# A two-layer graph attention kernel: separate buffers for background work, smaller stream tiles, a second list of late work

## The chip, the cores and the metric

The kernel runs on one core of a Trainium2 chip. The metric is the device time of one execution in microseconds: 3223.64 us as the median of three runs of the kernel before (3218.17 to 3225.19). The profile is of an execution with a span of 3218.2 us.

## What is computed

There are N = 2708 nodes with 1024 features each and a dense 0/1 adjacency matrix of 2708 x 2708. Everything is float32. Both layers start from a normalized and rectified copy of x and add their result to x:

```python
# layer 0
h = max(layernorm(x), 0)
f, g = h @ Wf + bf, h @ Wg + bg
e = relu(f @ g.T)
attention = softmax(where(adj > 0, e, -9e15), axis=1)
x = x + attention @ (h @ W + bW)
# layer 1
h = max(layernorm(x), 0)
hw = h @ W1
e = leaky_relu(hw @ a1 + (hw @ a2).T, 0.2)
attention = softmax(where(adj > 0, e, -9e15), axis=1)
x = x + relu(attention @ hw)
```

## The kernel before

**Tiling.** The nodes are cut into 21 full tiles of 128 rows and a rest of 20; the tiles go in pairs (NQ = 10 pairs and one pair of left-overs, MONO and TINY). The columns of the attention matrix, which are the rows of the result, are cut into five panels p of 512 to 576 columns. For each panel of layer 0 the kernel forms B = (Wf Wg') applied to the panel's h (`project_q`), the scores of all nodes against the panel (`scores`), their softmax, the aggregation of h by the weights (`aggregate` for panel 0, `aggregate_quartered` for the others), and a product with W (`project`). Layer 1 needs no score products: it builds the weights from two vectors (`weights1`), then aggregates and projects in the same way.

**Seven products.** Each big matrix product is done by a scheme of seven half-size products (M1 to M7) in place of eight, at the price of sums and differences of blocks. `aggregate_quartered` applies the scheme a second time inside five of the seven products (`BY_QUARTERS`); those inner products are `product` at L1030 and read two things from memory: blocks of h (`hr_d`) and precomputed sums of quarter blocks (`hs2_d`, called hs_d in the profile, as `hs_d` of the scores is too). Each inner product reads one tile "hc2" of 640 KB (five blocks of 256 columns, 5 KB in each partition).

**Sums made in the background.** The sums of quarters are made by `put_quarters` (L381): a load of four blocks ("hq", 512 KB), four VectorE operations into a second tile ("hq2"), and a store. There are 25 such items in each layer (five products, NK = 5 blocks each). `sums_h` (L353) makes first-level sums of h in the same manner from two tiles "hr" per pair, in place. `prepare_W` (L1284) loads rows of W ("w_rows"), sums them and stores the sums to `wt_d`. `raise_max` (L1325) updates running column maxima of layer 1 from a mask tile loaded by `load_mask` ("maskl", a slot).

**Queues and orders.** All loads are issued on SyncE, held in program order by `load` (L137). All stores are issued on GpSimd. Background work is a list, `later`: an item has a price in microseconds of VectorE, an optional fetch (its load) and an action. The main loops call `behind(us)`, which earns credit (capped at twice `us`) and runs items while credit is positive; `one` first issues the fetches of the next `ahead[0]` items (2 for most of the program, 1 during the first aggregation), then the first item's action. `flush` runs the whole list. `scores` calls `behind` after M6, M5, M2, M7, once with double rate after M3, and once after M4 of the previous pair; its rate is 1.0 for panel 1 and 0.65 from panel 2 on. While `nc.hold` names VectorE, as in `scores`, its operations too keep program order.

**Buffers.** On-chip memory is drawn from pools. `slots` has 53 buffers of 576 columns (score tiles S, B, T1, masks and temporaries). `strm` has ten buffers of 5 KB in each partition, as large as the largest tile asked of it, and serves every stream: As (operands of the scores), hc and hc2, md, w, adj_i (adjacency blocks), hsT, hT (four tiles per panel, L674), and the background's hq, hq2, hr and w_rows. A new tile takes a buffer that is free or waits for the last access of an older one; for a tile that is stored, that is the landing of the store. Since SyncE keeps program order, a load that waits for its buffer holds back all later loads.

**Order of the work around the change.** Panel 0's scores run while h is still being made (`make_pairs`, tiles hsT in the stream pool). Then come project_q(1), with `sums_h` behind it, aggregate(0, 0), with `sums_h` and `prepare_W` behind it, and scores of panel 1, with the 25 quarter sums of layer 0 behind it. For p from 1 to 4 come project(0, p-1), aggregate_quartered(0, p), project_q(p+1) and scores(p+1). Finished rows of layer 0 put new items for layer 1 on `later`. Before the last projection of layer 0 stands a `flush()` (L1686). In layer 1, `take_shifts(p)` (L1766) flushes and then takes the column maxima.

Of the kernel before, what the change touches and what calls it, by code (L numbers as in the profile page):

```python
# [8 lines left out]
FP = mybir.dt.float32  # L9
# [9 lines left out]
P = 128  # L19
W = 512  # L20
# [5 lines left out]
M1, M5, M6, M7, M3, M2, M4 = range(7)  # L26
# [4 lines left out]
BY_SCORES = (M1, M6, M5, M2, M7, M3, M4)  # L31
# [26 lines left out]
def kernel(  # L58
# [19 lines left out]
    nc = InOrder(tc)  # L78
    N, D = x.shape
    NC = D // P  # L80
    NH = NC // 2
# [4 lines left out]
    NM = P // 2  # L86
# [38 lines left out]
    def slot(name, shape=(P, WX), dt=FP):  # L125
        return slots.tile(list(shape), dt, tag="slot", name=name)

    def stream(name, shape=(P, D), dt=FP):
        return strm.tile(list(shape), dt, tag="strm", name=name)

    def in_16(o, i):

# [4 lines left out]
    def load(o, i):  # L137
        for a, b in in_16(o, i):
            tc.keep_in_program_order(nc.sync.dma_start(a, b))  # L139

    def store(o, i):
        for a, b in in_16(o, i):
            nc.gpsimd.dma_start(a, b)  # L143
# [43 lines left out]
        (nc.vector.tensor_copy if flip[0] else nc.scalar.copy)(o, i)  # L187


    later, credit = [], [0.0]  # L190
    ahead = [5]

    def put(us, go, fetch=None, takes_psum=False, ready=None):
        later.append([us, fetch, go, takes_psum, ready])

    def one():
        for it in later[:ahead[0]]:
            if it[1]:
                it[1]()
                it[1] = None  # L200
        us, _, go = later.pop(0)[:3]
# [179 lines left out]
    def put_quarters(l, m, k):  # L381

        two = []

        def fetch():
            two.append(stream("hq", (P, 4, WH)))
            load(two[0], hr_d[l][:, m, :, :, k].rearrange("p h f c -> p (h f) c"))

        def go():
            a11, a12, a21, a22 = (two[0][:, i] for i in range(4))  # L390
            o = stream("hq2", (P, 4, WH))
            s1, s2, s3, s4 = (o[:, i] for i in range(4))
            add(s1, a21, a22)
            sub(s2, s1, a11)
            sub(s3, a11, a21)
            sub(s4, a12, s2)
            store(hs2_d[l][:, m, :, k], o)
            made_quarters[l, m] = made_quarters.get((l, m), 0) + 1
        put(1.7, go, fetch)

    def quarters_until(l, m):
        while made_quarters.get((l, m), 0) < NK:
            one()

    u = consts.tile([P, NC], FP, name="u")
    v = consts.tile([P, NC], FP, name="v")
# [101 lines left out]
            one()  # L508


    def load_rows(w, c, name):
        t = stream(name)
        load(t, w[c * P:(c + 1) * P, :])
        return t

# [152 lines left out]
    def project_q(p, then={}):  # L668

        w = width[p]  # L670
        h = w // 2
        halved = lambda t: [t.rearrange("p (c i) -> p c i", c=NH)[:, 2 * g:2 * g + 2] for g in range(2)]
        lo, hi = ((halved(t) for t in first_h) if p == 0 else
                  ([stream("hT", (P, 2, WX)) for _ in range(2)] for _ in range(2)))  # L674
        o = 0
        for t, n in pieces[p]:
            if p == 0:
                break
            for e, side in enumerate((lo, hi)):
                for g in range(2):  # L680
                    s, cs = side[g][:, :, o:o + n], slice(2 * g, 2 * g + 2)
                    if t == TINY:
                        nc.scalar.copy(s, tinyT[:, e, cs, :NY])
                    elif t == MONO:
                        load(s, hsl_d[:, e, cs, NM:])
                    else:
                        q, k = pair_of[t]
                        load(s, hs_d[q][:, (BY_SCORES.index(M4 if k else M2) if e else 7 if k else BY_SCORES.index(M1)), cs])
# [5 lines left out]
        for g in range(2):  # L694
            sub(lo[g][:, :, h:w], hi[g][:, :, h:w], lo[g][:, :, h:w])

        def second():
            for g in range(2):
                sub(lo[g][:, :, :h], hi[g][:, :, h:w], T1[g][:, :, :h])

        def fourth():
            for g in range(2):
                sub(hi[g][:, :, :h], hi[g][:, :, :h], lo[g][:, :, :h])

        B = [in_pairs(f"B{m}") for m in range(7)]
        m1, m15, u2 = in_pairs("m1"), in_pairs("m15"), in_pairs("u2")
# [13 lines left out]
            return L[m][k][:, d * P:(d + 1) * P]  # L720

        def right(m, k):
            t, s = {M1: (lo, lo_), M2: (hi, lo_), M3: (hi, hi_), M5: (T1, lo_), M6: (lo, lo_), M7: (lo, hi_), M4: (hi, lo_)}[m]
            return t[k // 2][:, k % 2, s]

        def plus(o, a, bias, b):
            nc.vector.scalar_tensor_tensor(o, a, bias, b, op0=OP.add, op1=OP.add)
# [248 lines left out]
    def aggregate_quartered(l, p, S, sm, then={}, rate=3.0, fine=1.2):  # L976
# [33 lines left out]
            f_, b = i  # L1010
            return operand(m, 2 * k + f_)[:, b * hb:(b + 1) * hb]

        sums = {}

        def quarter_sums(m):

# [10 lines left out]
        def inner_right(m, n, k):  # L1027
            return sums[m, k][n] if n in sums[m, k] else part_of(m, k, {M1: (0, 0), M2: (1, 0), M3: (1, 1)}[n])

        def product(m, n, ps, start):  # L1030
            quarters_until(l, m)
            t = stream("hc2", (P, NK, WH))
            if n in (M1, M2, M4):
                load(t, hr_d[l][:, m, int(n == M4), int(n != M1)])
            else:
                load(t, hs2_d[l][:, m, {M5: 0, M6: 1, M7: 2, M3: 3}[n]])
            for k in range(NK):
                for d in range(2):
                    nc.tensor.matmul(ps[:, d], t[:, k, d * P:(d + 1) * P], inner_right(m, n, k),  # L1039
                                     start=(start and k == 0 and d == 0), stop=(k == NK - 1), skip_group_check=True)  # L1040
            behind(fine)

# [722 lines left out]

    def take_shifts(p):  # L1766
        flush()
        got["zm"] = shifts1(p)

    def take_weights(p):  # L1770
# [39 lines left out]
```

## Time and profile before

| What | Value |
|---|---|
| time, median of 3 | 3223.64 us |
| span of the profiled execution | 3218.2 us |
| mean granted TensorE clock | 0.973 |
| DMA traffic | 802.41 MB, mean 249 GB/s |
| hq loads and stores | 50 of 512 KB each; stores land 6.2 us after their issue (median) |
| hc2 loads | 280 of 640 KB |
| hT loads | 64 of 128 KB and 4 of 64 KB |

Each stage has its own limit. Busy time by stage, in microseconds, with the share of time in which the core's 16 DMA engines are busy:

| Stretch, us | Work | PE busy | VectorE busy | granted clock | DMA share |
|---|---|---|---|---|---|
| 212 to 372 | scores of panel 0 | 145.27 of 160 | 103.72 | 0.97 | 0.87 |
| 372 to 465 | project_q(1) | 73.67 of 93 | 68.80 | 0.89 | 0.72 |
| 465 to 640 | first aggregation | 156.98 of 175 | 92.75 | 0.97 | 0.86 |
| 640 to 860 | scores of panel 1 | 156.56 of 220 | 125.35 | 0.85 | 0.82 |
| 860 to 2145 | panels 1 to 4 of layer 0 | 1262.97 of 1285 | 930.37 | about 1 | about 0.83 |
| 2145 to 2262 | flush, last projection of layer 0 | 86.98 of 117 | 79.85 | 0.86 | 0.98 |
| 2262 to 3218 | layer 1 | 932.94 of 956.2 | 644.22 | 0.98 | about 0.73 |

In the page, PE is TensorE's matmuls, DVE is VectorE, ACT ScalarE, POOL GpSimd, and SP or SPq SyncE, whose instructions only issue transfers or wait. A line of waits names the engine, the tile and line that waited, what ended the wait, the total in microseconds, the number of times and the longest. A float32 matmul of the program appears as two in the profile, so one of the seven products of a pair in the scores, four matmuls in the code, shows as eight.

### The profile page before, as it was taken

The numbers are of one execution on the slowest core, as the hardware profiler recorded it, in microseconds if no ns is written. First come the engines' busy times: TensorE is split into PE (matmuls) and PEld (weight loads), VectorE is DVE, ScalarE is ACT, GpSimd is POOL, SyncE is SP. The second block draws the span as 40 slices with busy tenths as digits, with TensorE's granted clock in tenths as the row PEclk, the third lists the DMA queues.
The fourth block names the chain that finished last, engine by engine and source line by source line (L and its number), as shares of the span: only waits on it lengthen the run. The fifth ranks groups of instructions, "written<-read, shape, count | busy, mean of one in ns | idle before, by whom it ended". The sixth has DMA issues, their size and how long they took to land.

```text
span 3218.2 us, 43997 instructions
## 1 busy us (share of the span) xinstructions
PE 3014.6 (94%) x15606; PEld 2338.5 (73%) x15606; DVE 2184.8 (68%) x4956; ACT 478.5 (15%) x871; POOL 487.3 (15%) x704
## 2 busy tenths in 40 slices
PE   8998989866999999999999999996999999999998
PEld 4576667544669886788859887792765967969695
DVE  5765683655597466965688676985948567776853
ACT  3420020000030001200021000311313022131300
POOL 1420011211111001110041001112011011120102
PEclk9999999978999999999999999998999999999999
DMA  6999678888869787797778888799567757778787
GB/s 224 286 273 237 215 237 275 278 249 256 260 202 339 211 217 214 232 338 223 219 231 295 277 233 239 224 359 327 178 222 225 234 187 255 248 235 277 245 258 239
DMA packets 496714, 802.41 MB, mean 249 GB/s; under 512 B 175392, under 2 KB 330048, under 8 KB 496496
## 3 DMA queue, kind: packets, MB, share of 16 engines
q1 hardware_dynamic: 445136, 646.37, 65.4%
q0 software_dynamic: 51360, 153.24, 14.8%
q8 instruction: 124, 2.03, 0.3%
q14 instruction: 94, 0.77, 0.1%
HBM read 657.66 MB, written 141.78 MB: 248 GB/s over the span
## 4 chain that ended last, share of the span: by engine, by line
PE 63%; issue 16%; DMA 11%; DVE 5%; SPq 3%; POOL 2%; ACT 0%; POOLq 0%; DVEq 0%; ACTq 0%
PE sz L1365 7%; PE sx L1365 5%; PE gz L1039 5%; PE sy L1365 4%; PE pz L1246 4%; PE gy L646 4%; PE gx L646 4%; PE px L1246 3%; PE gy L1039 3%; PE gx L1039 3%; PE py L1246 3%; PE M_ps L559 3%; PE qz L646 3%; SPq L139 3%; PE qy L646 2%
## 5 line engine op out<-in xcount | busy, mean ns | idle before, releaser
L1365 PE MATMUL sz<-B,As 128*128 128x288 f32 (+2 forms) x1200 | 297.5, 398 | 10.6 <-DMA As<-hs_d 8.6
L1039 PE MATMUL gz<-quarter,hc 128*128 128x128 f32 (+2 forms) x2400 | 292.2, 279 | 6.7 <-DMA hc<-hs_d 4.5
L1039 PEld LDWEIGHTS gz<-quarter,hc 128*128 128x128 f32 x2400 | 282.4, 191 | 9.5 <-issue 5.0
L1365 PE MATMUL sx<-B,As 128*128 128x288 f32 (+2 forms) x800 | 214.5, 414 | 68.0 <-DMA As<-hs_d 63.6
L1365 PEld LDWEIGHTS sz<-B,As 128*128 128x128 f32 x1200 | 232.3, 194 | 60.4 <-issue 9.4
L1365 PEld LDWEIGHTS sx<-B,As 128*128 128x128 f32 x800 | 158.9, 200 | 107.0 <-DMA As<-hs_d 67.4
L1365 PE MATMUL sy<-B,As 128*128 128x288 f32 (+2 forms) x800 | 201.9, 396 | 3.4 <-DMA As<-hs_d 3.2
L646 PE MATMUL gy<-T,hc 128*128 128x288 f32 (+2 forms) x800 | 184.2, 391 | 0.0
L1365 PEld LDWEIGHTS sy<-B,As 128*128 128x128 f32 x800 | 153.6, 192 | 35.8 <-issue 3.9
L646 PEld LDWEIGHTS gy<-T,hc 128*128 128x128 f32 x800 | 152.0, 190 | 30.5
L1246 PE MATMUL px<-w,gT 128*128 128x512 f32 x320 | 143.6, 601 | 11.0 <-DMA w<-in_L_gnn_W_dram 11.0
L1246 PE MATMUL py<-w,ps 128*128 128x512 f32 x320 | 144.8, 602 | 6.0 <-issue 6.0
L1246 PE MATMUL pz<-w,ps 128*128 128x512 f32 x320 | 142.1, 594 | 0.8 <-DVE pt L45 0.8
L143 POOL DMA_DIRECT2D mk_d<-mask x55 | 36.1, 656 | 698.7 <-DVE mask L45 690.7
L1089 POOL TENSOR_TENSOR gT<-gT,rr 128x1024 f32<-128x1024 f32 (+5 forms) x16 | 61.0, 3813 | 531.7 <-DVE gT L45 531.7
L45 ACT COPY V<-gx 128x256 f32<-128x256 f32 (+2 forms) x80 | 30.4, 380 | 677.5 <-PE gx L1039 363.7
L45 DVE TENSOR_TENSOR V<-gz,V 128x256 f32<-128x256 f32 (+2 forms) x120 | 51.8, 432 | 115.3 <-PE gz L1039 115.1
L143 POOL DMA_DIRECT2D out_dram<-x_res x180 | 88.8, 500 | 242.5 <-DVE x_res L45 229.0
L45 ACT COPY sz<-sz 128x288 f32<-128x288 f32 (+2 forms) x5 | 1.9, 385 | 820.9 <-DVE acc L45 481.8
L1246 PEld LDWEIGHTS py<-w,ps 128*128 128x128 f32 x320 | 61.2, 193 | 82.7 <-issue 81.5
L1246 PEld LDWEIGHTS px<-w,gT 128*128 128x128 f32 x320 | 60.8, 193 | 82.7 <-issue 81.2
L1246 PEld LDWEIGHTS pz<-w,ps 128*128 128x128 f32 x320 | 60.2, 190 | 77.1 <-issue 71.6
(392 smaller groups left out, 5936.9 us busy)
## 6 DMA issues: line engine op xcount, KB each, us to landing
hc<-hs_d SPq DMA_DIRECT2D x160, 640.0 KB
As<-hs_d SPq DMA_DIRECT2D x150, 512.0 KB
hc<-hr_d SPq DMA_DIRECT2D x150, 512.0 KB
hc<-hr_d SPq DMA_DIRECT2D x120, 640.0 KB
w<-wt_d SPq DMA_DIRECT2D x96, 512.0 KB
w<-in_L_gnn_W_dram SPq DMA_DIRECT2D x72, 512.0 KB
md<-md_d SPq DMA_DIRECT2D x56, 512.0 KB
adj_i<-in_adj_dram SPq DMA_DIRECT2D x200, 128.0 KB
```

What stands on the lines that cost most here:

```text
L45: i = f(*a, **k)
L139: tc.keep_in_program_order(nc.sync.dma_start(a, b))
L143: nc.gpsimd.dma_start(a, b)
L559: nc.tensor.matmul(ps, wfT[a][c // NH][:, c % NH, :], wgT[b][c], start=(c == 0), stop=(c == NC - 1))
L646: nc.tensor.matmul(ps[d], left(m, k, d), right(m, k), start=(start and k == 0), stop=(k == K - 1), skip_group_check=True)
L1039: nc.tensor.matmul(ps[:, d], t[:, k, d * P:(d + 1) * P], inner_right(m, n, k), start=(start and k == 0 and d == 0), stop=(k == NK - 1), sk ...
L1089: nc.gpsimd.tensor_tensor(t, t, by(s, NH, k), OP.mult)
L1246: nc.tensor.matmul(ps, left[i][m][:, k, :], w_[k], start=(start and k == 0), stop=(k == NH - 1), skip_group_check=True)
L1365: nc.tensor.matmul(ps[:n, :h], lefts[q][:, i % 2, c, :n], B[m][c // 2][:, c % 2, :h], start=(start and c == 0), stop=(c == NH - 1), skip_g ...
```

## The change

Streams and background are to stop taking buffers from each other.

- A pool `side` of four buffers of 4 KB serves hq, hr and w_rows. The quarter sums are made in place, so that hq2 disappears.
- The stream pool goes from ten buffers of 5 KB to nine of 4 KB. For that the inner products' tile holds four of the five blocks, and the last block of all operands of a product m comes in two tiles "hl2" (one of `hr_d`, one of `hs2_d`) that live as long as m.
- hT of `project_q` moves from four stream tiles to eight slots, one for each half and 128 rows of features; its loads and subtractions become twice as many, of half the size.
- A second list `lazy` takes layer 1's quarter sums and the column maxima of panels 1 to 4. `behind` runs from it when `later` is empty, and `take_shifts` empties it; `flush` leaves it alone.

```diff
-    strm = ctx.enter_context(tc.tile_pool(name="strm", bufs=10))
+    strm = ctx.enter_context(tc.tile_pool(name="strm", bufs=9))
+    side = ctx.enter_context(tc.tile_pool(name="side", bufs=4))
...
-    def put(us, go, fetch=None, takes_psum=False, ready=None):
-        later.append([us, fetch, go, takes_psum, ready])
-
-    def one():
-        for it in later[:ahead[0]]:
+    def put(us, go, fetch=None, takes_psum=False, ready=None, to=later):
+        to.append([us, fetch, go, takes_psum, ready])
+
+    def one(of=None):
+        of = later if of is None else of
+        for it in of[:ahead[0]]:
...
         while later and credit[0] > 0 and (psum_free or not later[0][3]) and (not later[0][4] or later[0][4]()):
             credit[0] -= one()
+        while not later and lazy and credit[0] > 0:
+            credit[0] -= one(lazy)
...
-                two.append(stream("hr", (P, 2, W)))
+                two.append(aside("hr", (P, 2, W)))
...
-            two.append(stream("hq", (P, 4, WH)))
+            two.append(aside("hq", (P, 4, WH)))
...
-            o = stream("hq2", (P, 4, WH))
-            s1, s2, s3, s4 = (o[:, i] for i in range(4))
-            add(s1, a21, a22)
-            sub(s2, s1, a11)
-            sub(s3, a11, a21)
-            sub(s4, a12, s2)
-            store(hs2_d[l][:, m, :, k], o)
+            add(a22, a21, a22)
+            sub(a21, a11, a21)
+            sub(a11, a22, a11)
+            sub(a12, a12, a11)
+            store(hs2_d[l][:, m, :, k], two[0])
...
-        put(1.7, go, fetch)
+        put(1.7, go, fetch, to=lazy if l else later)
...
-        halved = lambda t: [t.rearrange("p (c i) -> p c i", c=NH)[:, 2 * g:2 * g + 2] for g in range(2)]
-        lo, hi = ((halved(t) for t in first_h) if p == 0 else
-                  ([stream("hT", (P, 2, WX)) for _ in range(2)] for _ in range(2)))
+        lo, hi = ([t[:, c * WX:(c + 1) * WX] for c in range(NH)] for t in first_h) if p == 0 else (
+            [slot(f"hT{e}{c}") for c in range(NH)] for e in range(2))
...
-        for g in range(2):
-            sub(T1[g][:, :, :h], lo[g][:, :, h:w], lo[g][:, :, :h])
+        for g in range(2):
+            for c in range(2):
+                sub(T1[g][:, c, :h], lo[2 * g + c][:, h:w], lo[2 * g + c][:, :h])
...
             quarters_until(l, m)
-            t = stream("hc2", (P, NK, WH))
-            if n in (M1, M2, M4):
-                load(t, hr_d[l][:, m, int(n == M4), int(n != M1)])
-            else:
-                load(t, hs2_d[l][:, m, {M5: 0, M6: 1, M7: 2, M3: 3}[n]])
+            if (m, 0) not in lasts:
+                for i, of in enumerate((hr_d[l][:, m, :, :, NK - 1].rearrange("p h f c -> p (h f) c"), hs2_d[l][:, m, :, NK - 1])):
+                    lasts[m, i] = stream("hl2", (P, 4, WH))
+                    load(lasts[m, i], of)
+            t = stream("hc2", (P, NK - 1, WH))
+            raw = n in (M1, M2, M4)
+            i = {M1: 0, M2: 1, M4: 3, M6: 0, M3: 1, M7: 2, M5: 3}[n]
+            load(t, hr_d[l][:, m, i // 2, i % 2, :NK - 1] if raw else hs2_d[l][:, m, i, :NK - 1])
+            last = lasts[m, int(not raw)][:, i]
...
-            rows[l, k] = [load_rows(w_in[l], c, "w_rows") for c in (k, k + NH)]
+            rows[l, k] = [load_rows(w_in[l], c, "w_rows", aside) for c in (k, k + NH)]
...
-                lambda k=k, mk=mk: mk.append(load_mask(p, q, k)))
+                lambda k=k, mk=mk: mk.append(load_mask(p, q, k)), to=lazy if p else later)
...
     def take_shifts(p):
         flush()
+        while lazy:
+            one(lazy)
         got["zm"] = shifts1(p)
```

More of the change, by code (lines that the diff above doesn't have):

```diff
@@ L129, in stream, with aside @@
         return strm.tile(list(shape), dt, tag="strm", name=name)
+    def aside(name, shape=(P, D), dt=FP):
+        return side.tile(list(shape), dt, tag="side", name=name)
     def in_16(o, i):
@@ L187, in copy @@
         (nc.vector.tensor_copy if flip[0] else nc.scalar.copy)(o, i)
-    later, credit = [], [0.0]
+    later, lazy, credit = [], [], [0.0]
     ahead = [5]
-    def put(us, go, fetch=None, takes_psum=False, ready=None):
-        later.append([us, fetch, go, takes_psum, ready])
-    def one():
-        for it in later[:ahead[0]]:
+    def put(us, go, fetch=None, takes_psum=False, ready=None, to=later):
[3 more added lines that the diff above has]
+        for it in of[:ahead[0]]:
             if it[1]:
@@ L200, in one @@
                 it[1] = None
-        us, _, go = later.pop(0)[:3]
+        us, _, go = of.pop(0)[:3]
         go()
@@ L390, in go @@
             a11, a12, a21, a22 = (two[0][:, i] for i in range(4))
-            o = stream("hq2", (P, 4, WH))
-            s1, s2, s3, s4 = (o[:, i] for i in range(4))
-            add(s1, a21, a22)
-            sub(s2, s1, a11)
-            sub(s3, a11, a21)
-            sub(s4, a12, s2)
-            store(hs2_d[l][:, m, :, k], o)
+            add(a22, a21, a22)
[3 more added lines that the diff above has]
+            store(hs2_d[l][:, m, :, k], two[0])
             made_quarters[l, m] = made_quarters.get((l, m), 0) + 1
-        put(1.7, go, fetch)
+        put(1.7, go, fetch, to=lazy if l else later)
     def quarters_until(l, m):
         while made_quarters.get((l, m), 0) < NK:
-            one()
+            one(lazy if l else later)
     u = consts.tile([P, NC], FP, name="u")
@@ L508, in make_until, with load_rows @@
             one()
-    def load_rows(w, c, name):
-        t = stream(name)
+    def load_rows(w, c, name, by=stream):
+        t = by(name)
         load(t, w[c * P:(c + 1) * P, :])
@@ L678, in project_q @@
                 break
-            for e, side in enumerate((lo, hi)):
-                for g in range(2):
-                    s, cs = side[g][:, :, o:o + n], slice(2 * g, 2 * g + 2)
+            for e, side_of in enumerate((lo, hi)):
+                for c in range(NH):
+                    s = side_of[c][:, o:o + n]
                     if t == TINY:
-                        nc.scalar.copy(s, tinyT[:, e, cs, :NY])
+                        nc.scalar.copy(s, tinyT[:, e, c, :NY])
                     elif t == MONO:
-                        load(s, hsl_d[:, e, cs, NM:])
+                        load(s, hsl_d[:, e, c, NM:])
                     else:
                         q, k = pair_of[t]
-                        load(s, hs_d[q][:, (BY_SCORES.index(M4 if k else M2) if e else 7 if k else BY_SCORES.index(M1)), cs])
+                        load(s, hs_d[q][:, (BY_SCORES.index(M4 if k else M2) if e else 7 if k else BY_SCORES.index(M1)), c])
             o += n
@@ L692, in project_q @@
         for g in range(2):
-            sub(T1[g][:, :, :h], lo[g][:, :, h:w], lo[g][:, :, :h])
-        for g in range(2):
-            sub(lo[g][:, :, h:w], hi[g][:, :, h:w], lo[g][:, :, h:w])
+            for c in range(2):
+                sub(T1[g][:, c, :h], lo[2 * g + c][:, h:w], lo[2 * g + c][:, :h])
+        for c in range(NH):
+            sub(lo[c][:, h:w], hi[c][:, h:w], lo[c][:, h:w])
         def second():
-            for g in range(2):
-                sub(lo[g][:, :, :h], hi[g][:, :, h:w], T1[g][:, :, :h])
+            for c in range(NH):
+                sub(lo[c][:, :h], hi[c][:, h:w], T1[c // 2][:, c % 2, :h])
         def fourth():
-            for g in range(2):
-                sub(hi[g][:, :, :h], hi[g][:, :, :h], lo[g][:, :, :h])
+            for c in range(NH):
+                sub(hi[c][:, :h], hi[c][:, :h], lo[c][:, :h])
         B = [in_pairs(f"B{m}") for m in range(7)]
@@ L722, in right @@
         def right(m, k):
-            t, s = {M1: (lo, lo_), M2: (hi, lo_), M3: (hi, hi_), M5: (T1, lo_), M6: (lo, lo_), M7: (lo, hi_), M4: (hi, lo_)}[m]
-            return t[k // 2][:, k % 2, s]
+            if m == M5:
+                return T1[k // 2][:, k % 2, :h]
+            t, s = {M1: (lo, lo_), M2: (hi, lo_), M3: (hi, hi_), M6: (lo, lo_), M7: (lo, hi_), M4: (hi, lo_)}[m]
+            return t[k][:, s]
         def plus(o, a, bias, b):
@@ L1011, in part_of @@
             return operand(m, 2 * k + f_)[:, b * hb:(b + 1) * hb]
-        sums = {}
+        sums, lasts = {}, {}
         def quarter_sums(m):
@@ L1031, in product @@
             quarters_until(l, m)
-            t = stream("hc2", (P, NK, WH))
-            if n in (M1, M2, M4):
-                load(t, hr_d[l][:, m, int(n == M4), int(n != M1)])
-            else:
-                load(t, hs2_d[l][:, m, {M5: 0, M6: 1, M7: 2, M3: 3}[n]])
+            if (m, 0) not in lasts:
[7 more added lines that the diff above has]
+            last = lasts[m, int(not raw)][:, i]
             for k in range(NK):
                 for d in range(2):
-                    nc.tensor.matmul(ps[:, d], t[:, k, d * P:(d + 1) * P], inner_right(m, n, k),
+                    lhs = t[:, k] if k < NK - 1 else last
+                    nc.tensor.matmul(ps[:, d], lhs[:, d * P:(d + 1) * P], inner_right(m, n, k),
                                      start=(start and k == 0 and d == 0), stop=(k == NK - 1), skip_group_check=True)
```

## The prediction

> **What bounds the kernel now.** I read the page's engine shares and slices first, then TensorE's waits stage by stage, then the SyncE timeline of the worst stage, because SyncE issues every load in program order.
>
> ```profile
> PE 3014.6 (94%) x15606; PEld 2338.5 (73%) x15606; DVE 2184.8 (68%) x4956; ACT 478.5 (15%) x871; POOL 487.3 (15%) x704
> ...
> PE   8998989866999999999999999996999999999998
> ```
>
> TensorE is busy for 3014.6 of 3218.2 us, and the change removes no matmul, so all it can win is in the 203.6 us that TensorE is idle. The slices put the idle time in the first third and around slice 27. TensorE's waits, cut to the stages, give the names (total, times, longest):
>
> ```profile
> PE sx L1365 <- DMA As<-hs_d: 60.7, 8, 12.1
> ...
> PE gz L646 <- DMA hc<-hr_d: 9.0, 2, 5.2
> ...
> PE px L1246 <- DMA w<-in_L_gnn_W_dram: 11.0, 1, 11.0
> PE mx_ps L839 <- DVE mx L45: 8.3, 1, 8.3
> PE py L1246 <- issue: 6.0, 1, 6.0
> ```
>
> The first line is 640 to 860 us (scores of panel 1, with the quarter sums of layer 0 behind it), the second 465 to 640 (first aggregation, with the rows of W behind it; 14.1 us of hc waits in all), the last three 2145 to 2262 (the flush and the last projection of layer 0). SyncE's timeline (start, length, issues) at the end of one round of the worst stage:
>
> ```profile
> 693.44 6.48 SPq L139 DMA_DIRECT2D hq<-hr_d  x2
> 700.01 3.01 SPq L139 DMA_DIRECT2D adj_i<-in_adj_dram  x4
> 703.07 3.95 SPq L139 DMA_DIRECT2D adj_t<-in_adj_dram  x4
> 707.12 1.30 SPq L139 DMA_DIRECT2D As<-hs_d  x2
> ```
>
> and TensorE's timeline there (start, length, engine, line, operation, count, idle time before):
>
> ```profile
> 713.24 4.21 PE L1365 MATMUL sx<-B,As 128*128 128x288 f32 x8 [12.07 <-DMA As<-hs_d]
> 717.24 4.12 PE L1365 MATMUL sz<-B,As 128*128 128x288 f32 x16
> ```
>
> Two issues of hq take 6.48 us where one issue takes 0.37: the second stands 5.7 us on "DMA hs_d<-hq" (16.3 us, 3 times, between 684 and 767). Eight adjacency issues follow (7.0 us), then As, which lands 6.1 us later, when TensorE has been idle 12.07 us.
>
> **What the Trainium skill says.** "DMA: Bandwidth & Descriptors", Anatomy of one DMA: semaphore waits happen on the issuing sequencer before dispatch. The trace agrees: the hq wait above holds back the adjacency and As loads, which need nothing from it. Same page, Issuing engines are not separate DMA queues: all DMAs run on the same 16 engines, so a pool of its own brings no bandwidth; the trace's queues together show a DMA share of 0.84 from 658 to 813 us. "TensorE: Matmul & The Clock Gate", Part 1: an idle window of about 3.4 us halves the clock. It agrees: after the 12.07 us gap eight matmuls take 4.21 us, elsewhere 2.10, so each such gap costs 2.1 us more.
>
> **The change, part by part.**
>
> A. *Quarter sums of layer 0 (25 items) in four side buffers, in place.* Four DVE operations of 0.42 us each before and after: nothing. A round of scores calls the filler with 7 credits and an item costs 1.7, so about four items run per round; the trace has 12 hq loads in the three rounds 684.7 to 766.6. Before, a round took 4 As + 1 adj_i + 8 hq/hq2 = 13 of ten buffers; after, 5 of nine, and 4 of the side's four. But follow the binding wait. An item is fetched one ahead of its turn; the round's first item runs behind M6, about 2 us after TensorE finishes it, and its store takes 6.2 us to land, so it frees its buffer at M6 + 6 (693.4 to 699.5 in the trace). The fourth fetch of the round, which stands directly ahead of the adjacency and As loads, is the fifth tile of a four-deep pool: **it waits for the very same store.** The sum is unchanged: 6.1 + 0.4 + 7.1 (adjacency) + 6.1 (As) = 19.7 us after M6, against four products of 1.94 = 7.8 of matmuls left: 11.9 us idle, measured 12.07. Waits on TensorE for As buffers (19.0 us on SyncE in the same stretch) go away but ended earlier than this one. I take 0; bounds: 5 us slower, 25 faster (rival 1).
>
> B. *Rows of W in the side pool.* Between 500 and 640 us SyncE stood 32.6 us on "DMA wt_d<-w_rows", mostly ahead of hc and As loads. Those waits go, but rows of item i now wait for item i-2's stores, and sixteen adjacency issues from 564 to 582 us stay ahead of one hc. Of 14.1 us of hc waits plus a 5.9 us As wait at 658: take 5 won, bounds -5 and 12.
>
> C. *Second list.* It holds layer 1's quarters and the column maxima of panels 1 to 4, and runs where the first is empty. The flush before the last projection of layer 0 now runs 20 maxima (15.8 us of DVE at 0.79, from 2158 to 2182) with their mask loads ahead of the W and x loads on SyncE. These are four tiles by five panels; four of the five panels leave, so 16 maxima: 12.6 us of DVE and 16 x 144 KB at most, about 6 us at the 366 GB/s of that stage. TensorE then waits 6.0 and 11.0 us; SyncE reaches the W loads at 2194.95 after 32 x issues that took 23.6 us with mask waits between them and 32 x 0.45 = 14.4 without. So about 10 of 17 us go, plus 2 us of half clock: 12 won, bounds 4 and 18. The maxima reappear in the first aggregation of layer 1 (2262 to 2424: DVE 113.9 busy of 162, so 12.6 fit) before its M3: 0, bounds -8 and 3; the 6.7 us hc wait there stays, since a fifth hq again waits for the first one's store.
>
> D. *Ten stream tiles become nine.* Where the side is not used this is a plain loss. In scores of panel 0 (212 to 372 us) transposed pairs and As tiles share the pool, nine per round; SyncE stood 39.6 us, 4 times, on "DMA hs_d<-hsT" and TensorE 14.7 us on As. One buffer less moves one As tile (two products, 3.9 us) behind such a store in each of three rounds: upper bound 12, lower 0; take 7.
>
> E. *hT in eight slots.* 16 loads of 128 KB become 32 of 64 KB (20 become 40 for panel 1), at 0.47 us per issue 7.5 us more ahead of the md loads, at four starts. Before they took 15.5 us (1423.53 to 1439.14), partly waiting for stream buffers, and TensorE waited 10.6 (panel 1, mostly behind hr), 1.0, 2.0 and 4.9 us. The stream waits go, and I count at most 51 of 53 slots in use at panel 1's start (22 score tiles, 14 of B, 8 hT, rb, acc and some 5 short-lived ones). DVE has 8 more subtractions, 1 us, beside M1. Take 4 lost in all, upper bound 30, lower -5. hr gains nothing: the third pair of sums_h waits for the first's store either way.
>
> F. *Last blocks apart.* Per product m nine loads of 512 KB replace seven of 640: 128 KB more, forty times. In layer 1 no DMA wait is shown inside these products (only 5.2 us on DVE), so nothing; in layer 0 DMA runs full (384 GB/s, 990 to 1040 us): 20 x 0.33 = 6.7 us upper bound, 0 lower. Two pinned tiles cut the lead to about seven loads, 17 us, above a landing. Take 2 lost; fewer tiles held by hq there win 1.
>
> Sum: -5 - 12 - 1 + 7 + 4 + 2 = -5, so **3219 us**. The likeliest is that the largest wait only changes the pool it is for.
>
> **Rivals.** (1) *The queue is freed.* If the fourth fetch does not wait (item order, or SyncE far enough ahead), a round is bounded by DMA: 154.7 us x 0.84 / 6 = 21.7 us per round instead of 25.8, six rounds, 25 us, plus half clocks and the 4.3 us at 813: 3188 us. For it: 13 tiles on ten buffers become 5 on nine. Against: the arithmetic in A. (2) *The shared buffers are missed*, ending slower: 12 (D, full) + 20 (E: md behind 7.5 us of issues at most starts) + 6 (F), against 12 won: 3250 us. For it: SyncE already issues back to back where hT loads, and the stream pool was exhausted in scores of panel 0. Against: TensorE waits only 1 to 5 us at these starts today.
>
> **How the numbers follow.** Likeliest case 0.5 (3219, spread 12), freed 0.25 (3188), missed buffers 0.25 (3250). Faster: 0.42 of the first and all of the second, 0.46; within 0.2%: a third of the first, 0.18; slower 0.36. The range takes both rivals' values and a little beyond: 3180 to 3252.
>
> **What would show it.** A: "PE sx <- DMA As" between 640 and 860 us stays near 60, and hq on SyncE still waits about 5.7 us for "DMA hs_d<-hq" once per round; under 30 us refutes it. B: "wt_d<-w_rows" on SyncE falls below 15 us. C: no maxima between 2150 and 2185 us of the old timeline, W's wait there 5 to 8 us instead of 17. D: As waits of panel 0 rise from 14.7 to about 22. E: md waits at the four project_q starts rise from about 18 to 22; over 40 is rival 2. F: hc waits inside quartered products stay under 15 us.

## The result, and the profile after

The changed kernel takes 3266.23 us (median; 3261.38 to 3269.6) where the kernel before takes 3220.98 us beside it (3218.17 to 3225.19). The ratio is 1.0138, interval 1.0119 to 1.0158: **slower by 1.4%**. The prediction said 3219, range 3180 to 3252: it forecast a slight gain, and the time lies above its range.

The page of the changed kernel, parts 1 and 2:

```profile
PE 3023.5 (93%) x15606; PEld 2348.6 (72%) x15606; DVE 2201.0 (68%) x4996; ACT 479.5 (15%) x875; POOL 488.2 (15%) x704
...
PE   8998889776999999989999799997899999999998
```

The matmuls are the same 15606. Their busy time grew by 8.9 us (3023.5 against 3014.6), the span by 41.4 us (3259.6 against 3218.2); the rest is new idle time. The slices give a first hint: the fifth and the eighth are a tenth lower than before, and there are new dips, 8 for 9 at slice 18 and 7 for 9 at slice 23 (1793 to 1874 us). The dip at 28 and 29 is that of slice 28 before, now across two. The lengths of the stages, each from its first matmul to the first of the next (a wait at the start of `project_q` therefore counts in the aggregation before it), were worked out from TensorE's timeline. Each is from one execution; kernels of the experiments below that share a stage's code and buffers differ there by up to 2 us, in the first aggregation by up to 4 and in scores of panel 0 by up to 5:

| Stage | before, us | after, us | difference |
|---|---|---|---|
| scores of panel 0 | 173.6 | 174.1 | +0.5 |
| project_q(1) | 79.3 | 83.7 | +4.4 |
| first aggregation | 172.7 | 187.8 | +15.1 |
| scores of panel 1 | 233.0 | 217.8 | -15.1 |
| quartered aggregations 1 to 4 of layer 0 | 138.2, 133.9, 134.2, 128.5 | 147.1, 145.5, 146.2, 132.4 | +36.4 |
| project_q(2) | 51.8 | 54.7 | +2.9 |
| last projection of layer 0 | 89.6 | 88.7 | -0.8 |
| all other stages together | | | -2 |

Three losses and one gain. **First aggregation:** SyncE's waits between 467 and 655 us of the changed kernel (total, times, longest):

```profile
SPq L143 <- DMA wt_d<-w_rows: 50.0, 8, 24.4
SPq L143 <- DMA hr_d<-hr: 38.9, 3, 29.1
```

Before, the same stretch had

```profile
SPq L139 <- DMA wt_d<-w_rows: 32.6, 6, 11.0
...
SPq L139 <- DMA hr_d<-hr: 16.9, 7, 7.6
```

SyncE's timeline of the changed kernel (start, length, engine, line, tile, issues) shows what stood behind them:

```profile
513.30 24.20 SPq L143 DMA_DIRECT2D hc<-hr_d  x8
537.60 34.66 SPq L143 DMA_DIRECT2D w_rows<-in_L_gnn_W_dram  x6
572.37 0.38 SPq L143 DMA_DIRECT2D hc<-hr_d  x1
```

TensorE's timeline at the same place:

```profile
579.58 10.20 PE L651 MATMUL gz<-Sa,hc 128*128 128x288 f32 x32 [8.59 <-DMA hc<-hr_d]
```

Six issues of w_rows took 34.66 us, most of it waiting for the stores of earlier rows; the hc behind them needed nothing from those stores, and TensorE stood 8.59 us.

**Starts of project_q:** SyncE's timeline ahead of the third of the four starts, before and after,

```profile
1423.53 15.51 SPq L139 DMA_DIRECT2D hT<-hs_d  x16
1439.14 0.89 SPq L139 DMA_DIRECT2D md<-md_d  x2
```

```profile
1445.37 19.53 SPq L143 DMA_DIRECT2D hT<-hs_d  x32
1465.00 0.86 SPq L143 DMA_DIRECT2D md<-md_d  x2
```

and TensorE's after:

```profile
1469.00 6.17 PE L651 MATMUL qx<-hT,md 128*128 128x256 f32 x14 [7.77 <-DMA md<-md_d]
```

SyncE now issues back to back, one hT in 0.61 us, and md comes after all 32. TensorE stands 7.77 us for md and then runs 14 matmuls in 6.17 us. The waits at the four starts add up to 43 us (18.1, 4.4, 7.8, 13.1), against 18.5 before (10.6, 1.0, 2.0, 4.9). At the first start it is eight issues of hr, 24.62 us from 380.11 on, that stand ahead of md.

**Scores of panel 1**, the gain. TensorE's waits between 655 and 873 us, and SyncE's timeline in one round:

```profile
PE sx L1377 <- DMA As<-hs_d: 53.5, 6, 11.2
```

```profile
748.26 12.65 SPq L143 DMA_DIRECT2D hq<-hr_d  x2
760.96 3.30 SPq L143 DMA_DIRECT2D adj_i<-in_adj_dram  x4
```

There are still five stalls of 10 to 11 us, each behind hq issues that wait (five of 11.3 to 12.4 us; the two issues shown take 12.65 us); before it was 60.7 us in eight. SyncE's waits for "DMA hs_d<-hq" in the stage even grew, from 36.9 to 74.9 us.

### The profile page after: what moved, and what is told of

It reads as the page before. It is cut to its first block, busy times and chain, and to the rows that moved or that the text cites. A ratio compares the mean times of both kernels' runs of the same rounds, so it can differ in the third digit from the quotient of the medians.

```text
span 3259.6 us, 44215 instructions
## 1 busy us (share of the span) xinstructions
PE 3023.5 (93%) x15606; PEld 2348.6 (72%) x15606; DVE 2201.0 (68%) x4996; ACT 479.5 (15%) x875; POOL 488.2 (15%) x704
## 3 DMA queue, kind: packets, MB, share of 16 engines
q0 software_dynamic: 51360, 153.24, 14.6%
## 4 chain that ended last, share of the span: by engine, by line
PE 66%; issue 12%; DMA 11%; DVE 5%; SPq 3%; POOL 2%; ACT 0%; POOLq 0%; DVEq 0%; ACTq 0%
PE sz L1377 7%; PE gz L1051 6%; PE pz L1258 5%; PE gy L651 5%; PE sx L1377 4%; PE sy L1377 4%; PE gx L1051 4%; PE px L1258 4%; PE gx L651 4%; PE gy L1051 4%; PE py L1258 4%; SPq L143 3%; PE M_ps L564 3%; PE qz L651 2%; DMA hc<-hr_d 2%
## 5 line engine op out<-in xcount | busy, mean ns | idle before, releaser
L1051 PE MATMUL gz<-quarter,hc 128*128 128x128 f32 (+2 forms) x1920 | 242.0, 279 | 4.1 <-DMA hc<-hs_d 2.0
L1051 PEld LDWEIGHTS gz<-quarter,hc 128*128 128x128 f32 x1920 | 230.2, 191 | 6.3 <-PE gz L1051 2.8
```

What stands on the lines that cost most here:

```text
L1051: nc.tensor.matmul(ps[:, d], lhs[:, d * P:(d + 1) * P], inner_right(m, n, k), start=(start and k == 0 and d == 0), stop=(k == NK - 1), ski ...
```

## The experiments

A ratio is always to the kernel before, timed on the same chip beside the kernel in question. The median of the kernel before was 3215.7 to 3223.5 us in these runs, so times of kernels from different runs compare only to within some 5 us. My theory was that **several independent costs** add up: the doubled hT issues, the pool of four as a new wait, the last blocks. The rival was **one cause, scarce stream buffers**: nine, of which two to four are pinned.

### Parts alone, on the kernel before

**hT in eight slots alone.** Edit:

```diff
-        lo, hi = ((halved(t) for t in first_h) if p == 0 else
-                  ([stream("hT", (P, 2, WX)) for _ in range(2)] for _ in range(2)))
+        lo, hi = ([t[:, c * WX:(c + 1) * WX] for c in range(NH)] for t in first_h) if p == 0 else (
+            [slot(f"hT{e}{c}") for c in range(NH)] for e in range(2))
```

> The kernel before with one part of the change: hT of q in eight 2 KB slots, loaded by 32 issues of 64 KB instead of 16 of 128 KB; ten stream buffers as before, no other part. Theory 'several costs' (the doubled issues stand ahead of the md loads at the four starts of project_q): 3235 to 3245 us, +15 to +25 over before, with md waits on TensorE of 30 us or more in all at the four starts (18.5 before). Rival 'scarce stream buffers' (everything lost comes from nine buffers of which two are pinned): 3216 to 3225, since here the eight tiles of hT only leave the stream pool and give it room.

Measured: 3237.15 us, ratio 1.0056 [1.0033, 1.0078], **+18 us** with all ten stream buffers and four tiles less in them. TensorE's waits at the four starts were 31.2 us (18.5 before), and the second and third quartered aggregations, as the table counts, grew by 7.5 and 7.1 us. Scarce stream buffers can't explain it.

**Last blocks apart alone.** Edit:

```diff
-            t = stream("hc2", (P, NK, WH))
+            if (m, 0) not in lasts:
...
+                    lasts[m, i] = stream("hl2", (P, 4, WH))
+                    load(lasts[m, i], of)
+            t = stream("hc2", (P, NK - 1, WH))
```

In this kernel the four sums of quarters are read in the changed kernel's order but stored in the old one, so sums are exchanged among products; loads, sizes and matmuls are those of the part.

> The kernel before with one part of the change: the fifth block of every quartered product's seven operands comes from two tiles per product, held through it, so nine loads in place of seven; ten stream buffers. Theory 'several costs': 3226 to 3234 us (+5 to +13), hc waits in the quartered products of layer 0 a few us longer. Rival 'scarce stream buffers': 3235 to 3245, since two pinned tiles of ten are what hurts and they are here in full. My prediction's own step F: +1 to +3.

Measured: 3264.2 us, 1.0149 [1.0125, 1.0174], **+48 us**. This is far above both expectations, and above my step F of +1. SyncE's timeline of this kernel at the start of a product m (hl are the pinned tiles):

```profile
980.40 0.36 SPq L139 DMA_DIRECT2D hl<-hr_d  x1
987.68 0.36 SPq L139 DMA_DIRECT2D hl<-hs_d  x1
988.13 0.93 SPq L139 DMA_DIRECT2D hc<-hr_d  x2
```

TensorE's timeline there:

```profile
992.99 4.18 PE L1044 MATMUL gx<-Sa,hc 128*128 128x144 f32 x16 [3.81 <-DMA hc<-hr_d]
```

The second pinned tile waits 6.9 us for a buffer, for "DMA hs_d<-hq" (SyncE's waits, 979 to 989 us). The hc behind it is issued at 988.13; TensorE wanted it at 992.99 - 3.81 = 989.18. The lead is one microsecond, and the 16 matmuls after the gap take 4.18 us where 16 of that shape took 2.20 after shorter gaps.

**The fifth block not held.** Two kernels load it by itself, next to each four-block tile, into 1 KB tiles of a pool of their own, and let it go after the product:

```diff
+            last = small.tile([P, WH], FP, tag="small", name="hl2")
+            load(last, of[:, NK - 1])
```

> The kernel before, where the fifth block of each quartered product's operand comes by a load of its own (14 loads for a product's seven operands, 64 to 128 KB the small ones) into a pool of four 1 KB tiles, let go right after the product. Ten stream buffers, none held. It has more issues and more small transfers than the last-blocks part (9 loads), but no stream buffer is pinned. Theory 'the two pinned buffers of ten cost the 48 us of that part alone': 3216 to 3228 here. Rival 'the extra issues and 1 KB packets cost it': 3255 or more.

Measured: 3250.52 us, 1.0085 [1.0069, 1.01], between the two. It settles nothing: four small tiles cap the lead at four products, and the waits of SyncE that "PE gx" ended, those for the small tiles among them, were 251.5 us, 113.5 before. So the next has ten, with hT in slots to make room (compare with 3237.15).

> The kernel before with hT in eight slots (as in the kernel with that part alone, 3237) and the fifth blocks by loads of their own into ten tiles of 1 KB, so that they never cap the lead of the ten stream buffers; none is held over products. Theory 'the held buffers of ten are what costs': 3235 to 3245, the four quartered aggregations of layer 0 within 2 us each of that kernel's 138.9, 141.4, 141.4, 127.7. Rival 'more issues and 1 KB packets cost it, held or not': 3255 to 3285, each of them 5 us longer or more.

Measured: 3230.43 us, 1.0024 [1.0015, 1.0032], no slower than its partner (1.0056 [1.0033, 1.0078]). The views by stretch over the four quartered aggregations of layer 0, their last line (us, then busy time of each engine): the kernel before, the last blocks held, and not held.

```profile
sum 534.80, PE 517.14 PEld 486.85 DVE 438.96 ACT 70.58 POOL 87.62; mean PE 129.28 PEld 121.71 DVE 109.74 ACT 17.64 POOL 21.91
```

```profile
sum 576.30, PE 531.76 PEld 500.17 DVE 443.70 ACT 70.84 POOL 87.83; mean PE 132.94 PEld 125.04 DVE 110.93 ACT 17.71 POOL 21.96
```

```profile
sum 550.50, PE 517.55 PEld 488.25 DVE 447.46 ACT 70.95 POOL 87.64; mean PE 129.39 PEld 122.06 DVE 111.87 ACT 17.74 POOL 21.91
```

Held: 41.5 us longer than before, 14.6 of it slower matmuls. Not held: 550.5, against 549.4 for its partner with hT alone. It has 14 loads per product m where the held form has nine, and about as many packets (538,126 and 538,955; 496,714 before). So **the two buffers taken out of ten are the cost**, and issues and small packets are none here. On this part the rival was right. Whether they cost by being held through m, or by being wanted at once at its start, was not told apart.

**The second list alone.** Edit:

```diff
-        put(1.7, go, fetch)
+        put(1.7, go, fetch, to=lazy if l else later)
...
-                lambda k=k, mk=mk: mk.append(load_mask(p, q, k)))
+                lambda k=k, mk=mk: mk.append(load_mask(p, q, k)), to=lazy if p else later)
```

> The kernel before with one part of the change: layer 1's quarter sums and the column maxima of panels 1 to 4 go to a second list that runs only when the first is empty. Step C of my prediction: 3207 to 3213 us (-8 to -14), the wait for W at the last projection of layer 0 drops from 17 to 5 to 8 us. Theory 'several costs', from the profile after (W wait 17.9 us, the x loads still take 23 us on SyncE without the mask loads): 3218 to 3224, no difference that can be told.

Measured: 3222.38 us, 1.0023 [1.0014, 1.0031]: +7 us, not -12. The wait for W was 18.2 us in one piece (17 us in two before). The quartered aggregations of layer 0 are 12 us longer together (546.9 against 534.8); why stays open.

**In-place sums alone**, in the shared pool of ten:

```diff
-            o = stream("hq2", (P, 4, WH))
...
+            add(a22, a21, a22)
+            sub(a21, a11, a21)
+            sub(a11, a22, a11)
+            sub(a12, a12, a11)
+            store(hs2_d[l][:, m, :, k], two[0])
```

> The kernel before with one part of the change: the quarter sums in place of the fetched tile (8 stream tiles less in a full round), in the shared pool of ten; no second pool, no other part. Theory 'in place is the good part, the split of the pools the bad one': a round takes 9 of ten buffers instead of 13; the As stalls of scores of panel 1 (67.3 us idle) fall to 30 to 45 as with one pool of 13: 3185 to 3202. Rival of my prediction ('another buffer's store is then waited for, the stall stays'): 3210 to 3221.

Measured: 3196.96 us, 0.992 [0.9904, 0.9937], **-25 us**. Its waits between 640 and 847 us:

```profile
PE sx L1363 <- DMA As<-hs_d: 31.8, 8, 9.3
PE sz L1363 <- DMA As<-hs_d: 8.4, 3, 5.6
```

The stage went from 233.0 to 207.2 us. My prediction's rival 1 (3188, the queue is freed) comes close here: ten buffers hold a round's nine tiles, and a fifth sum can take any of them that is free.

### The pool of four

**One pool of 13**, the same 52 KB, everything else as changed:

```diff
-    strm = ctx.enter_context(tc.tile_pool(name="strm", bufs=9))
-    side = ctx.enter_context(tc.tile_pool(name="side", bufs=4))
+    strm = ctx.enter_context(tc.tile_pool(name="strm", bufs=13))
```

> The changed kernel without the pool of four: one stream pool of 13 buffers of 4 KB takes everything (the quarter sums stay in place, all else as changed). Theory 'the pool of four is the new wait': the first aggregation loses its 15 us (hr and w_rows no longer wait for each other), the hc waits in layer 0's quartered products shrink by about 10 us, and the rounds of scores of panel 1 shorten since a fifth quarter sum finds a free buffer: 3266 - 15 - 10 - 20 = about 3220 us, 3205 to 3235. Rival 'issues on SyncE, not buffers': 3255 to 3265, as the queue stays as full whichever pool the tiles are from.

Measured: 3171.31 us, 0.9863 [0.9842, 0.9885]. **The split alone costs about 90 us** (3266.23 against 3171.31 is 95; by the ratios it is 89), twice what I expected. By stage against the changed kernel: scores of panel 1 -28.6, first aggregation -23.5, project_q(1) -9.3, first aggregation of layer 1 -8.0, scores of panel 0 -5.9, quartered aggregations -15.3 together. SyncE's waits in the first aggregation (454 to 618 us):

```profile
SPq L139 <- DMA wt_d<-w_rows: 24.3, 6, 7.1
...
SPq L139 <- DMA hr_d<-hr: 12.7, 5, 5.2
```

50.0 and 38.9 became 24.3 and 12.7, the longest 7.1 instead of 29.1. And by stretch, scores of panel 1 (us, busy times, then granted clock, DMA share and GB/s) in this kernel:

```profile
618.10:807.30 189.20, 162.82 (x645) 122.21 (x644) 132.57 (x291) 1.39 (x3) 34.82 (x44) 0.92 0.96 302
```

and in the changed one:

```profile
655.50:873.40 217.90, 162.54 (x646) 122.94 (x645) 132.81 (x291) 1.39 (x3) 33.81 (x43) 0.86 0.84 256
```

The same work, at a DMA share of 0.96 and not 0.84: with SyncE's waits for "DMA hs_d<-hq" down from 74.9 to 21.8 us, the transfers themselves fill nearly the whole stage.

**hr and the rows of W back** in the nine stream buffers; the pool of four keeps the quarter sums.

```diff
-                two.append(aside("hr", (P, 2, W)))
+                two.append(stream("hr", (P, 2, W)))
...
-            rows[l, k] = [load_rows(w_in[l], c, "w_rows", aside) for c in (k, k + NH)]
+            rows[l, k] = [load_rows(w_in[l], c, "w_rows") for c in (k, k + NH)]
```

> The changed kernel with hr and the rows of W taken from the nine stream buffers again; the pool of four holds only quarter sums. Theory 'in the pool of four hr and the rows of W wait for each other's stores' (SyncE stood 38.9 us on hr and 50.0 us on the rows of W in the first aggregation): that stage goes from 187.8 to 170 to 178 us, the rest as changed: 3266 - 13 = about 3253. Rival 'it only moves the wait to the nine stream buffers': stage 183 to 192, total 3260 to 3272.

Measured: 3244.87 us, 1.007 [1.005, 1.0089]. The first aggregation went from 187.8 to 174.5 us, as expected, and project_q(1) from 83.7 to 74.1, which I had not reckoned with: hr is background there too.

**Eight and five** in place of nine and four:

```diff
-    strm = ctx.enter_context(tc.tile_pool(name="strm", bufs=9))
-    side = ctx.enter_context(tc.tile_pool(name="side", bufs=4))
+    strm = ctx.enter_context(tc.tile_pool(name="strm", bufs=8))
+    side = ctx.enter_context(tc.tile_pool(name="side", bufs=5))
```

> The changed kernel with eight stream buffers and five in the side pool instead of nine and four. My step A said that a fifth fetch of quarter sums waits for the store of the first one because the pool is four deep. If that is what binds, the rounds of scores of panel 1 lose their 10 to 11 us stall down to about 5 (five rounds): that stage 217.8 -> about 190 us, and the first aggregation some us shorter (hr and rows of W wait less); against it the eighth stream buffer costs 5 to 20 us in layer 0's quartered products: 3245 us, 3230 to 3260. Rival 'any deep pool would stall there, DMA is full': stage at 213 to 220, total 3268 to 3285.

Measured: 3246.96 us, 1.0076 [1.0061, 1.0091]. Its waits in scores of panel 1 (655 to 851 us) and of panel 0 (211 to 398):

```profile
PE sx L1377 <- DMA As<-hs_d: 31.2, 6, 9.7
```

```profile
PE sx L1377 <- DMA As<-hs_d: 27.7, 3, 11.6
```

A fifth buffer takes 22.7 us off scores of panel 1 (217.8 to 195.1): step A's arithmetic, the fifth tile of a four-deep pool, is what sets that stall. Going from nine stream buffers to eight costs 12.6 us in scores of panel 0 (174.1 to 186.7), where going from ten to nine had cost nothing beyond the spread of that stage.

### hT's issues

**Loads of a tile pair joined**: 16 issues of two 64 KB runs into the same eight slots.

```diff
+                    elif pair_of[t][1] == 0:
+                        two = side_of[c][:, o:o + 2 * n].rearrange("p (k i) -> p k i", k=2)
+                        load(two, hs_d[pair_of[t][0]][:, 3:7:3, c] if e else hs_d[pair_of[t][0]][:, 0:8:7, c])
```

> The changed kernel with the hT loads of the two tiles of a pair joined again: 16 issues of 128 KB (two runs of 64 KB each) into the same eight slots. Theory 'the 16 extra issues of 0.5 to 0.6 us stand ahead of md': md waits at the four starts fall from 42.9 us to about 15, aggregations 2 and 3 each 7 us shorter: 3266 - 17 = about 3249, 3243 to 3254. Rival 'the start of the hT loads, not their number' (they begin only when the slots come free): 3261 to 3267, md waits stay near 40.

Measured: 3252.22 us, 1.0095 [1.0079, 1.0111], 14 us less than the changed kernel. SyncE's and then TensorE's timeline at the third panel's start:

```profile
1444.89 12.47 SPq L143 DMA_DIRECT2D hT<-hs_d  x16
1457.46 0.89 SPq L143 DMA_DIRECT2D md<-md_d  x2
```

```profile
1463.80 2.47 PE L651 MATMUL qx<-hT,md 128*128 128x256 f32 x5 [3.10 <-DMA md<-md_d]
```

The same bytes take 12.47 us of SyncE and not 19.53, md is issued 7 us sooner, and TensorE waits 3.10 instead of 7.77 us. The number of issues is the cost: during the 32 the DMA engines were busy 0.56 of the time (180 GB/s), during the 16 it was 0.90 (287 GB/s), so it was not the transfers that held SyncE. An issue has no fixed price, though: in the version kept at the end 16 of them take 15.04 us, at a DMA share of 0.91. At the first start 17.3 of 18.1 us stay; hr and the rows of W taken back left 4.5 us there, so those belong to the pool of four.

### W behind x

**Four W blocks ahead of x** at the last projection of layer 0:

```diff
-        ws = {m: load_W(l, m) for m in order[:2]}
+        ws = {m: load_W(l, m) for m in order[:4 if (l, p) == (0, NP - 1) else 2]}
```

> The changed kernel, where the last projection of layer 0 loads the W blocks of its first four products ahead of its 32 x tiles instead of those of the first two. Theory 'W is late because it stands behind 32 x issues, which take 23 us with the mask loads or without': the one wait of 17.9 us for W at that projection falls below 3, and the half clock after it goes as well: 3246 to 3250. Rival 'x and W share the DMA engines, W would land no earlier': 3260 to 3268.

Measured: 3267.39 us, 1.0135 [1.0111, 1.0159]: a miss, no change. TensorE's timeline:

```profile
2257.47 2.05 PE L1258 MATMUL py<-w,ps 128*128 128x512 f32 x2 [23.06 <-DMA w<-in_L_gnn_W_dram]
```

The wait moved two products on and grew: counted from the projection's first matmul, the x issues began 0.6 us after it, and in the changed kernel 3.8 before it.

**x in two lots**, the second pair's 16 issues after the first pair's W:

```diff
-        start_of([t for g in todo for t in g[:2]] + ([other] if other else []))
+        late = by_pair and (l, p) == (0, NP - 1)
+        start_of([t for g in (todo[:1] if late else todo) for t in g[:2]] + ([other] if other else []))
...
+                if late and m == M4 and j + 1 < len(todo):
+                    start_of(list(todo[j + 1][:2]))
```

> The changed kernel, where the last projection of layer 0 issues the x tiles of its second pair of tiles only after the W blocks of the first pair: 16 x issues instead of 32 stand ahead of the third W block. Theory 'W waits for the length of the block of x issues ahead of it on SyncE (0.7 us each)': the wait of 17.9 us falls by 16 x 0.7 = 11 to 5 to 8 us, total 3266 - 12 = about 3254 (3250 to 3258). Rival 'the wait has another source, such as the DMA engines or the stream buffers': it stays above 14 and the total within 4 of 3266.

Measured: 3271.9 us, 1.016 [1.0137, 1.0183]. The first wait fell as the theory said, but the other half came back:

```profile
2237.37 5.98 PE L1259 MATMUL px<-w,gT 128*128 128x512 f32 x8 [7.68 <-DMA w<-in_L_gnn_W_dram]
...
2263.29 6.67 PE L1259 MATMUL px<-w,gT 128*128 128x512 f32 x8 [5.15 <-DMA w<-in_L_gnn_W_dram]
```

Its idle time is 19.4 us as in the changed kernel (19.0), in more pieces, and after each the eight matmuls take about 6 us or more instead of 3.60; the projection is 93.9 and not 88.7 us. W does wait behind x, but reordering only places the wait. Whether the count of x issues or their transfers set it was not tried.

### Together

> All that gained, together: the changed kernel with one stream pool of 13 instead of nine and four, hT loads of a tile pair joined, four W blocks ahead of the x tiles at the last projection of layer 0. If the parts add up: 3171 - 14 - 17 = about 3140. If one wait was only hiding another: 3155 to 3165.

Measured: 3147.89 us, 0.9766 [0.9742, 0.979], between the two expectations.

> The changed kernel with only two edits: one stream pool of 13, and the hT loads of a tile pair joined; W and x at the last projection of layer 0 as in the change. If these two carry the whole gain of the best kernel so far (3147.9, which also loads four W blocks ahead): 3144 to 3152. If the four W blocks ahead had their part in it: 3156 to 3166.

Measured: **3146.68 us, 0.9773 [0.9747, 0.9799]**. These two edits carry all of it, and this is the version to keep: 2.3% below the kernel before. Joining the hT loads took 14 us off the changed kernel and 25 off that with one pool: project_q(1), whose start waits for hr in the changed kernel, stays at 83.8 us there and goes from 74.5 to 65.3 with one pool. The page's part 1 of this version:

```profile
PE 2999.7 (95%) x15606; PEld 2334.9 (74%) x15606; DVE 2197.0 (70%) x4996; ACT 478.5 (15%) x875; POOL 487.3 (16%) x704
```

Three variants of it were no better. x in two lots (without the four W blocks):

> The best kernel so far (one pool of 13, hT loads of a tile pair joined) with the x tiles in two lots instead of the four W blocks ahead: the wait of 21.6 us for W falls to about 8: 3147.9 - 13 = about 3135, 3130 to 3142. Rival: no change, 3144 to 3152.

Measured: 3153.19 us, 0.979 [0.9767, 0.9812]; its last projection is 94.9 us long against 91.0, as above. The same with one list:

> The kernel of the run before in this list without the second list: layer 1's quarter sums and all maxima in one list again. If the second list costs by itself, as it did alone on the kernel before (+6.7): 3128 (about 7 less than its partner). If it cost there only because ten shared buffers were scarce: within 3 of its partner. If it helps once there are buffers (step C of my prediction): 5 to 12 more than its partner.

Measured: 3157.85 us, 0.9811 [0.979, 0.9832]; the intervals overlap with its partner's, so with 13 buffers the second list makes no difference that this shows. The same with the fifth block not held, in eight 1 KB tiles, and 11 stream buffers:

> The same partner with the fifth blocks in eight tiles of 1 KB of their own, let go after each product, and 11 stream buffers instead of 13 (the same memory). Theory 'holding two of the stream buffers costs, issues do not': 11 buffers of which none is held equal 13 of which two to four are: between -8 and +2 of its partner. Rival 'the number of issues': +10 or more.

Measured: 3169.53 us, 0.9842 [0.9818, 0.9865], 16 us more than its partner: the rival's number, but not for its reason. The quartered aggregations of layer 0 are shorter (-4.8, -0.9, -1.0, -1.8), so by these lengths holding costs some 8 us even with 13, and more issues cost nothing; but two buffers less cost 10.7 us in the first aggregation and 8.2 in project_q(1).

## Why the prediction was wrong

**A, right in mechanism, 15 us off in size.** The fourth fetch of a round does wait for the first one's store (in the round shown that store lands at 760.49 us and the second hq goes out at 760.54), and five stalls stayed, as eight and five buffers confirm. But the stage is 15.1 us shorter: 7.2 us less of As waits (60.7 to 53.5), and 6.9 us less of matmuls (169.46 to 162.54 busy in the stage), which run slow after each gap and had fewer of them. The larger lesson was in the rival that I had at 0.25: in place in the shared pool wins 25 us; it is the pool of four that kept the wait.

**B, wrong sign.** The step said -5. It measured +15.1 in the first aggregation, and 13.2 of that leave with hr and the rows of W. The failing sentence is "those waits go, but rows of item i now wait for item i-2's stores": I saw the new wait and sized it below the old one. It is not one landing long, but reaches from the fetch to the landing. Of the six w_rows issues above, four went out by 539.74 and filled the pool. VectorE's timeline there:

```profile
560.35 0.46 DVE L45 TENSOR_TENSOR m<-gy,m 128x288 f32<-128x288 f32 x1 [15.96 <-PE gy L651]
...
562.67 0.68 DVE L45 TENSOR_TENSOR wT<-w_rows 128x512 f32<-128x512 f32 x1
```

It stood 15.96 us for TensorE's gy and came to the sums of the rows only at 562.67; the first store landed at 566.96, and the fifth issue went out at 567.02. I also left out that hr draws on the same four tiles, two per item; its longest wait was 29.1 us. The run took both back at once, so their shares are not told apart. My check value, w_rows below 15 us on SyncE, measured 50.0.

**C, wrong.** -12 forecast, +7 alone, about 0 at the last projection of the changed kernel (-0.8). The failing number is "32 x 0.45 = 14.4 without": in the changed kernel the four lots of x issues take 7.59 + 3.70 + 5.12 + 5.02 = 21.4 us with 1.3 us of mask issues between them. The masks had not been what delayed x, and the profile before had shown it: 7.80 + 3.64 + 5.41 + 5.07 = 21.9 us for the same four lots.

**D, not seen.** +7 forecast; TensorE's waits for As in scores of panel 0 were 14.7 us with ten and 12.6 with nine. The loss starts at eight (27.7 us).

**E, right in mechanism, mis-sized.** +4 forecast with a bound of 30; alone +18, and joining the loads recovers 14. The 43 us at the four starts are above the 40 that I had named as the sign of rival 2, but most of the 18.1 at the first start comes from hr and not from hT. I had the 7.5 us per start, and then let TensorE's small waits of 1 to 5 us stand as slack. They were none: a start that already waits has none. The Trainium skill, "Perfetto Trace Analysis", What "DMA-bound" means, lists a solid issuing sequencer as a bound of its own; SyncE's 19.53 us without a gap is that. "DMA: Bandwidth & Descriptors", Anatomy of one DMA, says, of the GpSimd path, that many descriptors can be emitted before their cost shows; that is not a price of issues on SyncE, where 16 more took 7 us here.

**F, the worst.** +1 net forecast, +48 alone. The failing step is "Two pinned tiles cut the lead to about seven loads, 17 us, above a landing". The quarter sums drew on that pool too: in the stretch shown above, their stores and the pinned tiles together brought the lead down to 1 us. In the changed kernel hq is elsewhere, and F's part is smaller. Of the 36.4 us of its quartered aggregations 15.3 go with one pool of 13 and 14.2 more with the joined hT loads; 6.9 stay, and not holding the last blocks takes 8.5 off in the kernel with one pool.

Worked out by stage, A -15, B +15 and +4 in project_q(1), E, F and the waits of the pool of four +39 (with project_q(2)), the rest -2 make +41, the difference of the spans. Both theories had a part: hT is a cost of issues, the last blocks one of scarce buffers. Rival 2 of the prediction (3250) had the right direction, and its 20 for E was near the +18 of that part alone. Otherwise it came near by luck: its 12 for D and its 12 won did not come, its 6 for F were the price of bytes and not of held buffers, and B's loss is not in it.

## What to carry to other kernels

A pool cut off for background work must be deep enough for the whole time from a fetch to the landing of its store, times the users it has; otherwise its wait is the old one under a new name, and with one in-order load queue it still stops the main stream. Sharing the same memory in one pool was worth about 90 us here, spread over the stages. Before tiles are held across products, count the lead that is left in the stage where stores hold buffers too, and before a load is split, ask what stands next in the queue.

## What the hardware showed unexpectedly

40,300 more packets and seven more loads for every product cost nothing (550.5 against 549.4 us over four stages) where the lead was kept, while 16 more issues ahead of one awaited load cost 7 us, with the DMA engines busy only 0.56 of that time. And what a gap costs beyond itself is large: after stalls of 5 to 8 us, eight matmuls of 128x512 took 6.0 to 6.7 us against 3.60.
